# A four-layer vision network on one core: set-up spread out, statistics taken early, norms in steps, and both Toeplitz operands copied in pieces of eight channels

## The chip, the cores and the metric

The kernel runs on one core of one Trainium2 chip. The metric is the device time in microseconds (us) of that core for the whole program. A core has a matrix engine (PE, with its weight loads PEld), a vector engine (DVE), a scalar engine (ACT), a general engine (POOL) and a queue engine that only issues transfers (SP). The profile covers one execution of the same program.

## What is computed

The input is eight images of 56 x 56 positions and 192 channels, all in float32. Four layers follow one another, each of the form `x = x + layer(group_norm(x))`, where the group norm has 32 groups of six channels per image.

```python
# layer 0: gated Toeplitz mixing, 576 inner channels
p, q, v = silu(x @ p_w.T + p_b), silu(x @ q_w.T + q_b), silu(x @ v_w.T + v_b)
a1, a2 = rpe_mlp1(lag) * decay, rpe_mlp2(lag) * decay      # one value per lag and channel
o1 = toeplitz(q * v along w, a1);  o2 = toeplitz(q * v along h, a2)
layer0 = (p * (o1 + o2)) @ o_w.T + o_b
# layer 1: layer norm, then shifted 7 x 7 window attention, 6 heads, bias table and mask
# layer 2: x @ W_in, depthwise 3 x 3, four exponential scans, layer norm, @ W_out
# layer 3: depthwise 7 x 7, layer norm, @ w0, gelu, @ w1, times a small scale
```

A Toeplitz mix of one channel is a 56 x 56 matrix, whose entry depends only on the lag w - w', times a 56 x 56 image of q*v. So layer 0 is 576 pairs of small products per image, one for each direction.

## The kernel before

An image sits in SBUF as 128 partitions: two halves of 28 rows, 64 partitions each, with three chunks of 64 channels in the free dimension (`[128, 3, 1568]`). The program is a row of stages, each over all eight images, and what passes from stage to stage goes through DRAM.

**q and v** (`layer0_qv`, L318 on). For each of 14 slots of an image: matmuls with `w_qv` (L331), bias on DVE (L337), Silu on ACT (L338), product on DVE (L339), and six stores of q*v into two DRAM tables `left` and `right` in runs of 64 channels, or 256 bytes (L342, L347). Group norm of the next image is `layer0_in` (L309): DVE statistics (L149), two small matmuls over the groups (L164), a square root on ACT, and the scaling `xn` (L315). Set-up happens before and between the slots: `toeplitz_rows` (L209) computes the lag coefficients, and each of its 18 blocks reads them back as a sliding window (`hk`, L262, runs of 56 values), reverses them on DVE (`tzt`, L265) and stores them as 64 Toeplitz rows in `left` or `right` (L266). `build_bias_mask` (L271) gathers the bias table with 42 tiny transfers (L280) ahead of the first slot and writes eight mask blocks. The framework that builds the program settles the order of instructions on each engine itself. The trace shows it: the text spreads the 18 blocks over six images, yet the 18 `tzt` copies lie between 77 and 421 us, and only at 422 us is the norm of the fourth image made.

**Mixing** (`layer0_mix`, L442). A block is 64 channels of one image; per image there are nine. Its left and right operands (`lt`, `rt`, 1.79 MB each, L363) stack the Toeplitz rows and the q*v rows so that one product over 128 partitions yields o1 + o2 of one channel. A row holds position and channel, `w * 64 + d`, so the 56 values of one channel lie 64 values (256 bytes) apart. `layer0_operands` (L353) copies the left operand on POOL into `lc`, where a channel is contiguous, in halves of 32 channels (L368); the right operand is read where it lies:

```python
rc = raw[1].rearrange("p (w u d) -> p u d w", u=nu, d=64 // nu)[:, :, nh * q:nh * q + nh]
nc.tensor.matmul(op[64*u:64*u + W, i, :], lc[:, nh*u + d0 + i], rc[:, u, d0 + i], start=True, stop=True)
```

`layer0_products` (L375) does eight products (x `nu`, the number of output halves used together: 2 in eight blocks of an image, 1 in the ninth), and copies them out of PSUM, in turn on DVE (L396) and ACT (L394). After each eight, `between` lets the gate of the pass before go on (`layer0_gate`, L399): p-projection `pj` (L409), Silu (L414), transposes `ot` (L420), gate product (L423), output projection `y` (L430), and the addition into x (L436, L438).

**Layer 1.** `layer1_load` (L547) brings an image in, shifted, in 18 transfers of short runs. `layer1_norm` (L552) is a generator whose first step takes the group statistics of the image; its further steps run between scores and mixing of the image before, by `plan`. `layer1_scores` and `layer1_mix` follow for four groups of windows; the last addition is L717.

**Layer 2.** `layer2_in` (L720): load, statistics (L149, 420 columns at a time), `xn` (L735), 90 matmuls with `w_in` (L747), bias on DVE (L755), one store. `layer2_mix` does the convolution and scans (L791, L806, L807, L815). The output stage takes layer-norm statistics (`ln_pieces`, L187), scales (L862, L864), transposes (L868), projects (`layer2_out`, L883, L888), and after each quarter gives `layer3_in` (L891) a step: statistics of the finished image, norm (`zp`, L900), transposes (L920) and copies (L912, L914).

**Layer 3.** `convolve` (L936) is the 7 x 7 convolution (L956). `layer3_out` (L972) for one image: load `yl`, bias on POOL (L979), 28 layer-norm statistics on DVE (L187), square root on ACT (L202), scaling (L993), transposes (L1000), copy on ACT (L1011), then four rounds of `ph` (L1019), Gelu on ACT (L1023), `po` (L1028), scale on ACT (L1033) and addition (L1035).

Of the kernel before, what the change touches and what calls it, by code (L numbers as in the profile page):

```python
# [76 lines left out]
def kernel(ctx: ExitStack, tc: tile.TileContext, a: dict, out: bass.AP):  # L77
# [43 lines left out]

    left, right = (dram.tile([(nimg * W + 64) * NSUB, QR], F32, name=n) for n in ("left", "right"))
# [15 lines left out]
    def gn_stats_halves(x, pool, psum, sc, sh, ptag="qv"):  # L138

        gn_finish(gn_pieces(x, pool), x.shape[2], pool, psum, sc, sh, ptag)  # L140

    def gn_pieces(x, pool):
        n = x.shape[2]
        nt = -(-n // 512)
        st = pool.tile([128, 3, nt, 6], F32, name="gh_st")
        mv = pool.tile([128, 3, 2], F32, name="gh_mv")
        for j in range(3):
            for t in range(nt):
                nc.vector.bn_stats(st[:, j, t, :], x[:, j, bass.ts(t, n // nt)])  # L149
            nc.vector.bn_aggr(mv[:, j, :], st[:, j].rearrange("p t s -> p (t s)"))  # L150
        return mv

    def gn_finish(mv, n, pool, psum, sc, sh, ptag):
        def over_groups(v, name):
            if ptag == "mm":
                ps = psum.tile([128, 512], F32, name=name, tag="mm", bufs=3)[:, 0:3]
            elif ptag == "gn":
                ps = psum.tile([128, 3], F32, name=name, tag="gn", bufs=1)
            else:
                ps = psum.tile([128, 2, 512], F32, name=name, tag=ptag)[:, 0, 0:3]  # L160
            for j in range(3):
                ks = [k for k in range(3) if abs(j - k) < 2]
                for k in ks:
                    nc.tensor.matmul(ps[:, j:j + 1], gmath[:, k, j, :], v[:, k:k + 1], start=(k == ks[0]), stop=(k == ks[-1]))  # L164
            return ps


        mean = pool.tile([128, 3], F32, name="gh_mean")
        nc.vector.tensor_scalar(mean, over_groups(mv[:, :, 0], "gh_m"), n / NH, None, ALU.mult)
        d = pool.tile([128, 3], F32, name="gh_d")  # L170
        nc.vector.tensor_tensor(d, mv[:, :, 0], mean, ALU.subtract)
        nc.vector.tensor_tensor(d, d, d, ALU.mult)
        nc.vector.tensor_tensor(d, d, mv[:, :, 1], ALU.add)
        if n == NH:
            nc.scalar.activation(sc, over_groups(d, "gh_v"), AF.Sqrt, bias=eps5)
        else:

            z = pool.tile([128, 3], F32, name="gh_z")
            nc.vector.scalar_tensor_tensor(z, mean, 1.0 - n / NH, mean, ALU.mult, ALU.mult)
            nc.vector.scalar_tensor_tensor(z, over_groups(d, "gh_v"), n / NH, z, ALU.mult, ALU.add)  # L180
            nc.scalar.activation(sc, z, AF.Sqrt, bias=eps5)
# [1105 lines left out]
```

## Time and profile before

The time is 6748.18 us, the median of three (6744.67 to 6751.29); the profiled execution spans 6762.3 us. The stages, cut at their first and last matmuls in the trace, and the busy times of the windows that cover them:

| stage | from, to (us) | PE busy | what the windows show |
|---|---|---|---|
| set-up | 0 to 47 | | x arrives at 18, first q/v matmul at 46.7 |
| q and v | 47 to 935 | 765 of 888 us | transfers busy 0.82 to 0.98 of the time |
| mixing | 964 to 2324 | 399 to 400 of every 400 us | PE clock 1.00, POOL 129 to 151 of 400 us |
| layer 1 | 2324 to 3824 | 82 to 85% after the start | PE clock 0.83 to 0.88 |
| layer 2 in | 3824 to 4245 | 83% after the start | DVE 70% |
| layer 2 mix | 4245 to 4885 | nearly 100% | DVE 88% |
| layer 2 out, layer 3 in | 4885 to 5440 | 79 to 86% | DVE 80 to 85% in the first two of its three windows |
| convolution | 5460 to 5765 | | |
| layer 3 out | 5765 to 6762 | 107 of each 120 us in the middle | |

In the page, `busy` counts an engine's own instructions; a busy PE may still be slow per instruction. The forty digits of part 2 show in tenths how busy an engine was in each slice of 169 us. A `<-` names what ended a wait. In matmul rows of the trace a float32 product appears as two records, a transpose as one.

### The profile page before, as it was taken

The page shows a single profiled execution, that of the slowest core. Times are in us where ns is not written, and L with a number is a line of the kernel's source. Part 1 is how long each engine was busy: PE and PEld are TensorE (multiplying, and loading weights), DVE is VectorE, ACT ScalarE, POOL GpSimd, SP SyncE. Part 2 cuts the span into 40 slices and gives each one's busy share as a digit, 9 for nine tenths or more (in the row PEclk, how much of TensorE's full clock was granted, in tenths as well). Part 3 has the DMA queues.
Part 4 walks back from the last instruction along what each step waited for, and adds up shares of the span by engine and source line. Part 5 has one row for each costly group of instructions (what it writes and reads, how often), then busy time and mean ns, then how long its engine had stood idle before and what let it go on. Part 6 is the DMA issues. An engine that isn't in the chain of part 4 may idle for free. (4 is left out here: it accounts for less than half of the span.)

```text
span 6762.3 us, 126227 instructions
## 1 busy us (share of the span) xinstructions
PE 5845.8 (86%) x55962; PEld 3906.1 (58%) x55962; DVE 3297.8 (49%) x4694; ACT 1999.7 (30%) x2784; POOL 1301.5 (19%) x692
## 2 busy tenths in 40 slices
PE   6689989999999778888888588899868889698999
PEld 5567767777777544545454345577534479344444
DVE  6677753333333344444444276688788711532231
ACT  1234431111111133333333100355445410233333
POOL 4210023333333111122121100333301100101000
PEclk8889999999999888888888788999988889799999
DMA  8998895556655434444443554666666588221121
GB/s 193 209 194 176 164 278 206 225 225 225 225 226 224 104 55 59 52 57 53 48 57 44 71 159 164 211 227 233 192 176 191 157 306 318 96 82 51 53 67 26
DMA packets 1041747, 1027.69 MB, mean 152 GB/s; under 512 B 831196, under 2 KB 963716, under 8 KB 1014192
## 3 DMA queue, kind: packets, MB, share of 16 engines
q1 hardware_dynamic: 1028064, 954.30, 50.6%
q0 software_dynamic: 11408, 62.32, 3.7%
q8 instruction: 439, 7.19, 0.4%
q10 hardware_dynamic: 1728, 2.99, 0.1%
q14 instruction: 108, 0.88, 0.0%
HBM read 674.35 MB, written 345.07 MB: 151 GB/s over the span
## 5 line engine op out<-in xcount | busy, mean ns | idle before, releaser
L331 PE MATMUL qv<-w_qv_sb,xn 64*112 64x288 f32 x5376 | 736.1, 428 | 101.4 <-DVE act L337 101.1
L331 PEld LDWEIGHTS qv<-w_qv_sb,xn 64*112 64x112 f32 x5376 | 573.9, 185 | 260.9 <-DVE act L337 127.5
L368 POOL COPY lc<-lt 128x1792 f32<-128x1792 f32 x144 | 473.1, 3289 | 840.0 <-PE op L387 736.8
L387 PE MATMUL op<-rt,lc 128*56 128x56 f32 x9216 | 561.6, 275 | 3.1 <-DMA rt<-right 2.9
L387 PEld LDWEIGHTS op<-rt,lc 128*56 128x56 f32 x9216 | 507.8, 145 | 75.1 <-issue 58.7
L1028 PE MATMUL po<-hid,w_sb 128*64 128x392 f32 x2304 | 400.7, 506 | 69.0 <-ACT hid L1023 69.0
L338 ACT ACTIVATE act<-act 112x576 f32<-112x576 f32 x448 | 301.1, 683 | 507.3 <-DVE act L337 506.7
L1019 PE MATMUL ph<-y,w_sb 64*128 64x392 f32 x2304 | 421.9, 499 | 8.0 <-ACT hid L1023 8.0
L409 PE MATMUL pj<-xn,w_p_sb 64*128 64x392 f32 (+1 forms) x1920 | 370.5, 507 | 25.9 <-DVE xn L451 21.4
L1035 DVE TENSOR_TENSOR x<-x,z 128x392 f32<-128x392 f32 x96 | 54.5, 567 | 654.2 <-ACT z L1033 654.2
L430 PE MATMUL y<-pp,w_o_sb 128*64 128x392 f32 (+1 forms) x1920 | 353.3, 499 | 1.6 <-DVE pp L423 1.2
L423 DVE TENSOR_TENSOR pp<-pp,ot 128x784 f32<-128x784 f32 (+1 forms) x160 | 155.0, 969 | 403.4 <-ACT pp L414 396.3
L1028 PEld LDWEIGHTS po<-hid,w_sb 128*64 128x64 f32 x2304 | 165.6, 140 | 300.3 <-issue 224.6
L791 PE MATMUL cv<-zc,wt 128*128 128x224 f32 x1536 | 312.2, 355 | 28.6 <-DMA zc<-pd 28.6
L337 DVE TENSOR_TENSOR act<-qv,b_qv 112x576 f32<-112x576 f32 x448 | 317.3, 750 | 36.3 <-PE qv L331 36.3
L1019 PEld LDWEIGHTS ph<-y,w_sb 64*128 64x128 f32 x2304 | 232.4, 189 | 172.8 <-issue 25.8
L791 PEld LDWEIGHTS cv<-zc,wt 128*128 128x128 f32 x1536 | 289.9, 189 | 71.7 <-issue 55.9
L660 POOL TENSOR_TENSOR e<-e,mx 128x1176 f32<-128x1176 f32 x64 | 139.9, 2185 | 966.3 <-DVE mx L659 857.5
L610 PE MATMUL qk_ps<-xr,wg 64*96 64x392 f32 x1536 | 309.9, 512 | 14.1 <-ACT qk L616 10.8
L956 PE MATMUL cps<-zc,wt 128*128 128x224 f32 x1536 | 299.0, 355 | 23.4 <-DMA zc<-zd 22.6
L414 ACT ACTIVATE pp<-pj,vecs_sb 128x784 f32<-128x784 f32 (+1 forms) x160 | 146.3, 915 | 568.6 <-PE pj L409 566.5
L747 PE MATMUL pin<-w_in_sb,xn 64*128 64x384 f32 x1392 | 259.6, 521 | 56.9 <-POOL xn L738 36.8
(205 smaller groups left out, 9355.5 us busy)
## 6 DMA issues: line engine op xcount, KB each, us to landing
lt<-left SPq DMA_DIRECT2D x72, 1792.0 KB
rt<-right SPq DMA_DIRECT2D x72, 1792.0 KB
left<-qv SPq DMA_DIRECT2D x224, 252.0 KB
right<-qv SPq DMA_DIRECT2D x448, 126.0 KB
wt<-in_band_dram SPq DMA_DIRECT2D x24, 2048.0 KB
wt<-in_band_dram SPq DMA_DIRECT2D x12, 4096.0 KB
pd<-pt SPq DMA_DIRECT2D x8, 5568.0 KB
zc<-pd SPq DMA_DIRECT2D x192, 232.0 KB
```

The costliest lines, as they stand in the source:

```text
L331: nc.tensor.matmul(ps[s][:, which, 0:D1 // 2], xn[64 * s:64 * s + 64, j, bass.ts(i, 2 * W)], w_qv[64 * s:64 * s + 64, j, which, ns], start ...
L337: nc.vector.tensor_tensor(act, ps[s][:, :, 0:D1 // 2], b_qv[:, :, ns], ALU.add)
L338: nc.scalar.activation(act, act, AF.Silu)
L368: nc.gpsimd.tensor_copy(lc.rearrange("p (u d) w -> p u d w", u=nu), raw[0].rearrange("p (w u d) -> p u d w", u=nu, d=64 // nu)[:, :, nh * ...
L387: nc.tensor.matmul(op[64 * u:64 * u + W, i, :], lc[:, nh * u + d0 + i], rc[:, u, d0 + i], start=True, stop=True)
L409: nc.tensor.matmul(ps[0:M, s, 0:TT], w_p[64 * s:64 * s + 64, j, d0:d0 + M], xn[64 * s:64 * s + 64, j, ts], start=(j == 0), stop=(j == 2),)
L430: nc.tensor.matmul(y[64 * s:64 * s + 64], w_o[0:M, c, 64 * j:64 * j + 64], pp[0:M, s], start=(c == gated[0][0]), stop=(c == gated[-1][0]),)
L610: nc.tensor.matmul(ps[s], wg[64 * s:64 * s + 64, j, c0:c0 + HC], xw[64 * s:64 * s + 64, j, gs], start=(j == 0), stop=(j == 2),)
L791: nc.tensor.matmul(dst, wt[:, c4 + i, 128 * q:128 * q + 128], zc[:, :, c4 + i, q:q + NPAIR], start=(q == 0), stop=(q == 1),)
L956: nc.tensor.matmul(dst.rearrange("p (b n) -> p b n", n=NPAIR), wt[:, c4 + i, q * OP:(q + 1) * OP], zc[:, :, c4 + i, q:q + NPAIR], start=(q ...
L1019: nc.tensor.matmul(ps[:, s, 0:TT], w0[64 * s:64 * s + 64, j, m * 128:(m + 1) * 128], y[64 * s:64 * s + 64, j, ts], start=(j == 0), stop=(j ...
L1028: nc.tensor.matmul(ps[64 * s:64 * s + 64], w1[:, m, 64 * j:64 * j + 64], hid[:, m, s], start=(m == 0), stop=(m == 5),)
```

## The change

The change has four parts.

1. **Set-up spread.** The lag coefficients are computed by a generator, two steps a slot, in image 0. They are transposed on PE and stored in DRAM with the lag as the slow dimension and 64 channels contiguous, so that a Toeplitz row is one contiguous run of 56 x 64 values. The `hk`/`tzt` blocks are gone: 112 transfers from DRAM to DRAM (nine runs of 14,336 bytes each) make the rows and 16 make the zero rows, all issued by ACT, one or two per slot. The bias table's 42 transfers move to slot 10 of image 0 and the eight mask blocks to later slots.
2. **Statistics early.** The group statistics of layer 1 are taken by `gn_piece` in layer 0's last gate, those of layer 2 after each of layer 1's four `layer1_mix` calls; the group averages of seven images come in one call, the eighth's in another. `layer1_norm` and `layer2_in` then only read scale and shift. Layer 1's first two images are loaded before the last gate of layer 0, and the raw operand buffers stand on the other side of SBUF so that they are there before the q/v stage ends.
3. **Norms in steps.** `layer3_in` is cut into more steps, given after each projection chunk of `layer2_out`; the layer-norm pieces are spread likewise. `layer3_out` is split: `layer3_norm` of the next image is a generator, given a step after every second Gelu of the current image, and its variance (DVE) and its square root (ACT) are separate steps. Loads run an image further ahead.
4. **Both operands copied.** The right operand is copied as well, now in pieces of eight channels (x `nu`), in turn on DVE and ACT (`rc`, three buffers); the left operand stays on POOL, in the same pieces (`lc`, two buffers).

The core of the diff:

```diff
-            hk = pool.tile([W, 64, W], F32, name="hk")
-            nc.gpsimd.dma_start(hk, bass.AP(src.tensor, src.offset, [[1, W], [112, 64], [1, W]]))
-            nc.vector.tensor_copy(_reversed(tz[0:W].rearrange("p w d -> p d w")), hk)
-            nc.gpsimd.dma_start((left, right)[i][toep_row(s):toep_row(s) + 64], tz.rearrange("p w d -> p (w d)"))
+        def row(i, w0):
+            nc.scalar.dma_start(
+                parts[i][w0], coef[i][:, 55 - w0:111 - w0].rearrange("s l d -> s (l d)")
+            )
+        def zeros(i, k):
+            nc.scalar.dma_start(parts[i][k], none.partition_broadcast(NSUB))
...
-        nc.gpsimd.tensor_copy(
-            lc.rearrange("p (u d) w -> p u d w", u=nu),
-            raw[0].rearrange("p (w u d) -> p u d w", u=nu, d=64 // nu)[:, :, nh * q:nh * q + nh],
-        )
-        rc = raw[1].rearrange("p (w u d) -> p u d w", u=nu, d=64 // nu)[:, :, nh * q:nh * q + nh]
+    def layer0_operand(copy, raw, name, bufs, d0, nu, pool):
+        c = pool.tile([128, 2, 8, W], F32, name=name, bufs=bufs)
+        copy(c[:, 0:nu], raw.rearrange("p (w u d) -> p u d w", u=nu, d=64 // nu)[:, :, d0:d0 + 8])
+        return c
...
+                for at in range(0, 64 // nu * len(subs), 8):
+                    right_operand()
+                    layer0_products(ops[n % 2], nu, lcs[n], rcs[n])
+                    left_operand()
+                    part = 64 * (nu - 1) + W
+                    copies[n % 2](o[0:part, :, at:at + 8], ops[n % 2][0:part].rearrange("p d h -> p h d"))
+                    n += 1
+                    between()
...
+            if g == len(PASSES) - 1:
+                gn_piece(st, x, t)
+        loaded()
...
-        gn_stats_halves(x.rearrange("p j h w -> p j (h w)"), pool, psum, sc, sh, "mm")
-        yield
+        sc, sh = scsh1[:, b, 0], scsh1[:, b, 1]
...
-        gn_stats_halves(x.rearrange("p j h w -> p j (h w)"), pool, psum, sc, sh, "pin")
+        sc, sh = scsh2[:, b, 0], scsh2[:, b, 1]
...
+        for n in range(0, NPAIR, 4):
+            yield
+            ln_pieces(st, yl, range(n, n + 4))
+        rows = ln_var(st, OP, C, pool)
+        yield
+        rs, mr = ln_rows(*rows, OP, eps6, pool)
         for i0 in range(0, PH, 4):
+            yield
...
                 nc.scalar.activation(hid[:, m], ps[:, :, 0:TT], AF.Gelu, bias=vec("b0", m))
+                if m % 2:
+                    between()
```

## The prediction

> **What bounds the kernel now.** I read the page's slices first, then windows stage by stage, because each stage has its own limit.
>
> ```profile
> PE   6689989999999778888888588899868889698999
> PEclk8889999999999888888888788999988889799999
> DMA  8998895556655434444443554666666588221121
> ```
>
> PE is above 80% nearly everywhere, so what counts is where PE waits and how fast its instructions are. The windows (an image of q/v with Toeplitz blocks, one without, mixing, layer 2 in, layer 3 out) show the stages:
>
> ```profile
> core 0: us, PE busy (x) PEld busy (x) DVE busy (x) ACT busy (x) POOL busy (x), PEclk, DMA share, GB/s
> 111.00:272.00 161.00, 109.16 (x688) 87.47 (x686) 101.82 (x158) 40.46 (x59) 45.37 (x26) 0.84 0.97 202
> 422.00:521.00 99.00, 92.77 (x704) 69.34 (x702) 74.42 (x137) 40.47 (x59) 0.75 (x2) 0.93 0.90 192
> 1000.00:1400.00 400.00, 398.57 (x4556) 293.63 (x4558) 131.07 (x185) 67.05 (x93) 143.18 (x44) 1.00 0.61 235
> 3895.00:4050.00 155.00, 128.07 (x702) 78.10 (x704) 110.22 (x143) 0.89 (x3) 7.60 (x18) 0.86 0.57 173
> 5944.00:6064.00 120.00, 107.14 (x617) 53.84 (x615) 34.98 (x76) 40.23 (x51) 10.35 (x4) 0.94 0.19 64
> ```
>
> An image of q/v lasts 161 us with transfers busy at 0.97, 99 us without blocks. Mixing is PE alone. In the other two PE has gaps; the list of waits on PE names them:
>
> ```profile
> PE gh_m L164 <- DVE gh_mv L150: 113.4, 7, 57.0
> PE qv L331 <- DVE act L337: 101.1, 27, 17.3
> PE po L1028 <- ACT hid L1023: 69.0, 6, 11.9
> PE gh_v L164 <- DVE gh_d L173: 68.6, 23, 7.7
> ```
>
> Two are group-norm chains. The third is a queue effect, in the timeline of layer 3 out:
>
> ```profile
> 5977.78 0.32 ACT L202 ACTIVATE ln_rs<-ln_var,eps 128x28 f32<-128x28 f32 x1 [13.64 <-DVE ln_var L200]
> ...
> 5980.38 0.92 PE L1028 MATMUL po<-hid,w_sb 128*64 128x392 f32 x2 [11.76 <-ACT hid L1023]
> ```
>
> The square root for the next image stands in ACT's queue ahead of a Gelu and waits 13.6 us for its variance; PE waits 11.8 us behind it.
>
> For mixing I looked at the products (PE's timeline, with two outputs in turn, then with one):
>
> ```profile
> 1472.05 3.34 PE L387 MATMUL op<-rt,lc 128*56 128x56 f32 x64
> 1475.32 0.88 PE L430 MATMUL y<-pp,w_o_sb 64*64 64x392 f32 x4
> ...
> 1611.32 1.72 PE L387 MATMUL op<-rt,lc 128*56 128x56 f32 x16
> 1612.96 1.26 PE L409 MATMUL pj<-xn,w_p_sb 64*128 64x392 f32 x6
> ```
>
> From start to next start: 3.27/64 = 51 ns a record in pairs, 1.64/16 = 102 ns alone. The convolution L956 has 256 records in 49.5 us, 193 ns for 224 columns that lie in runs, 0.86 ns a column; at that rate 56 columns take 48 ns. Alone they take twice that, and only the right operand is read at a stride.
>
> **What the Trainium skill says.** "Advanced Engine Details and Errata", section Memory Cachelines: SBUF lines are 16 bytes and a read that meets a new line each time is penalized. The trace agrees: 102 against 48 ns at a 256-byte step. "TensorE: Matmul & The Clock Gate", section LDWEIGHTS: a weight load takes its columns / 1.2 ns, 107 ns for 128; the 14 `gh_m` records of 128 columns and one moving column took 1.72 us, 123 ns each, which fits. By it 56 columns take 47 ns, a possible floor (estimate). "SBUF — State Buffer", section on the two sides: POOL and a DVE copy in its fast mode lock each other out for a whole instruction. The trace fits: L315 takes 1.09 us alone, and one group of three 5.96 us. "DMA: Bandwidth & Descriptors", section on why a DMA increments by 16: the number of engines is the largest divisor up to 16 of the slowest dimension. A row transfer has nine; no transfer before shows it.
>
> **The change, part by part.**
>
> *Set-up and q/v (0 to 935).* The coefficient chain and bias table leave the path to the first matmul: `xn` ends at 35.8, the first matmul is at 46.7. The blocks' sliding reads (18 x 784 KB in 224-byte runs) and `tzt` (18 x 3.23 = 58 us of DVE) go. Images without blocks took 99, 96, 96 and 88 us, and the last 23 slots 134.4, which is 82 per 14. Added are 128 transfers of 126 KB each, issued by ACT. An ACT issue took about 0.45 us at the start and 0.9 for `coef`: 58 to 115 us on ACT, which is busy 320 of 888; Silu waits behind it, DVE's product behind Silu. As transfer time: 16.5 MB on nine of 16 engines; the loads `lt` and `rt` ran at up to 384 GB/s on 16 (window 935 to 1000), so 24 GB/s an engine gives 76 us over the stage, 10 an image, on engines that are 0.83 to 0.9 busy already. I take 98 an image: 36 + 7 x 98 + 82 = 804, rounded to 810: **-125** (-145 if the transfers hide, -20 if they don't). The mask blocks are only moved; they hide in DVE's 25% slack. Operands loaded early shorten the 29 us to the first product: **-10**.
>
> *Products.* With both operands contiguous, one record alone should take max(48, weights 47) plus the transposes' 10 ns of overhead, 57. In pairs PE ran two column groups at once (51 = 102/2); the bounds are 28 (half of 57) and 49 (weight loads in a row). The nearest row, `v_ps` with 64-column weights in four quadrants, has 94 records in 2.30 us, 24 ns, which a strict row of loads within a row group (53/2 = 27) would not allow. I take 35. Pairs: 8192 records x 16 = -132. Alone: 1024 x 45 = -46. The copies: 320 pieces, 896 values in pairs. POOL's 3289 ns for 1792 gives 1.65 each, 256 x 1.65 + 64 x 0.9 = 480 us as before. On DVE 0.9 ns a value (`tzt`) to 2.0 (`zt`, 1084 for 512): 0.8 to 1.8 us; ACT likewise (`zt` 1090). 160 pieces each add 130 to 290 us to DVE's 452 and to ACT's 233: both below the new stage of 1200. But `lc` has two buffers: piece n+2 can be copied only after products n; and DVE copies queue ahead of the gate's L423, behind which `y` on PE waits, with shorter products to cover it. 160 gate chunks x 0.25 us = +40. Net **-138**.
>
> *Statistics early.* Layer 1's start (2324 to 2418): x arrives at 2359, stats and chain end at 2373; both now lie under the last gate: **-48**. In its body 28 matmuls an image go (3.4 us of PE, and some 1.6 of waits), seven times: **-35**; DVE trades one set of 12 statistics for another. Layer 2 in: an image takes 43.9 us ((4243+3-3895)/8), PE's matmuls 174 x 0.161 = 28, DVE's additions 15 x 1.53 = 23 plus 3.3 for `xn`. Without 12 x 0.575 of statistics and the chain (PE idle or on `gh` from 3931 to 3942) PE bounds it at 30: **-105**, and the first chain **-12**; its load still waits for the 18 stores (SP issues for 40 us).
>
> *Steps.* Layer 2 out: about 66 us an image, DVE 53, PE 52. ACT waited 13.4 us for `gh_v` in one image, PE 6.7 for `gh_d`. Nothing is removed; I take 60: **-50** (0 to -75). Layer 3 out: the last image, whose norm was made before, takes 105. Five images fall from 120 to 104.5 and the first from 138: **-110**. DVE (35 us an image) and ACT (40) have room.
>
> Sum: -125 -10 -138 -48 -35 -105 -12 -50 -110 = -633; 6748 - 633 = **6115**.
>
> **Rivals.** *Weight loads bound the products*: pairs stay at 49, saving 17 + 46 - 40 = 23 instead of 138: 6230. For it, the 123 ns of `gh_m`; against it, `v_ps`. *Transfers still bound q/v*: nine engines get all rows, or ACT's queue holds up Silu: -20 instead of -125, 6220. For it, 0.90 without blocks. *Everything overlaps*: pairs at 28 with no give-back (-230 instead of -138), q/v -145, layer 2 out -75, and some 15 more from the rest: 5960. *Slower*: the buffers make mixing a series. A group of 1.1 us of products, then a left copy that waits for a DVE copy (1.65 + 1.85), then its gate (104 us an image / 40 = 2.6) is 7.2 us x 320 = 2300 instead of 1358: +942 against -495 of the rest: 7195. For it, the shared port and two buffers; against it, POOL is busy only 36% and a gate step lies between most groups.
>
> **The numbers.** The forecast 0.45, weight loads 0.18, transfers 0.12, everything 0.18, slower 0.07. The range runs from the best case to the weight-load case plus 80 for the open sizes of the steps: 5960 to 6310. Faster 0.92, same 0.01, slower 0.07.
>
> **What would show it.** The first L331 near 36; q/v images near 98 with transfers near 0.9; L387 at 35 ns a record in pairs and 57 alone, with PE still at 0.95 or more in mixing; no `gh` rows in layer 1's and layer 2's images; L747 every 30 us; no ACT wait for `ln_var` and 104 us an image at the end. It would be wrong if PE waits for `rc` or `lc`, if pairs stay near 50, or if ACT's queue stands in its own transfers.

## The result and the profile after

The changed kernel takes 6349.33 us (median of 6344.86 to 6358.06), the kernel before 6749.74 beside it: a ratio of 0.9408, 95% interval 0.9392 to 0.9425. That is 400 us less, where the prediction had 633 and ended its range at 6310. The direction held and the size did not. Cut at the same first and last matmuls as before, the profiled spans (6762.3 and 6349.2) divide like this:

| term of the prediction | before (us) | after (us) | forecast | measured |
|---|---|---|---|---|
| set-up and q/v, 0 to the last `qv` | 935.2 | 867.3 | -125 | **-68** |
| last `qv` to the first product | 29.3 | 7.7 | -10 | -22 |
| mixing, first to last product | 1331.6 | 1194.4 | -138 | -137 |
| layer 1 start, last product to first `qk` | 121.5 | 100.2 | -48 | **-21** |
| layer 1, first `qk` to last `pr` | 1405.9 | 1387.6 | -35 | -18 |
| last `pr` to the first `pin` | 71.3 | 56.1 | -12 | -15 |
| layer 2 in, first to last `pin` | 348.2 | 242.8 | -105 | -105 |
| layer 2 out, first to last `po` | 475.5 | 475.8 | -50 | **0** |
| layer 3 out, first `ph` to last `po` | 948.5 | 923.9 | -110 | **-25** |

Part 2 of the page of the changed kernel, the span in 40 slices (of 159 us now):

```profile
PE   6799989999999688888888598999588798789999
PEclk8899999999999888888888799999798799899999
DMA  6799886666665613444433675666667488121211
```

The windows answer to those shown of before: an image of q/v in which mask blocks are made, one late in the stage, mixing, layer 2 in, layer 3 out. The columns are the window, its length, the busy time of the five engine rows, the PE clock, the transfers' busy share and GB/s.

```profile
core 0: us, PE busy (x) PEld busy (x) DVE busy (x) ACT busy (x) POOL busy (x), PEclk, DMA share, GB/s
228.00:325.00 97.00, 71.30 (x439) 59.16 (x441) 56.37 (x131) 24.43 (x37) 17.02 (x29) 0.81 0.69 168
616.00:713.00 97.00, 95.58 (x762) 71.42 (x760) 73.85 (x132) 43.83 (x65) 0.00 (x0) 0.96 0.93 207
1300.00:1700.00 400.00, 379.53 (x5190) 249.76 (x5188) 244.81 (x312) 166.92 (x163) 201.80 (x110) 0.98 0.71 267
3613.00:3768.00 155.00, 154.67 (x912) 109.47 (x913) 129.85 (x95) 0.00 (x0) 13.19 (x31) 0.98 0.88 264
5770.00:5885.00 115.00, 107.89 (x620) 53.78 (x619) 35.18 (x77) 40.01 (x51) 10.71 (x4) 0.96 0.20 67
```

Late in q/v PE is full with the transfers at 0.93, and layer 2 in is bound by PE, as forecast. Three rows are not as forecast. In the first, PE is idle for a quarter of the time and DVE, ACT and transfers are all less busy than in the second: something makes them wait for one another. In mixing PE is no longer full (0.95), and its clock is 0.98. In layer 3 out PE has 107.9 of 115 us.

The list of waits on PE puts names to the idle time (total, times, longest):

```profile
PE ph L1087 <- ACT hid L1091: 49.1, 6, 10.0
PE qv L366 <- DVE act L372: 47.6, 19, 5.5
PE po L926 <- DVE x2o L931: 46.1, 8, 9.8
```

The second was 101.1 before. Waits for `hid` were 69.0 before, at `po`, and should have gone; in the prediction's words "no ACT wait for `ln_var`". The third was 17.6: it has grown. Each is read in a timeline below.

The products, from PE's timeline, first with one output, then with two in turn:

```profile
1310.64 0.99 PE L412 MATMUL op<-rc,lc 128*56 128x56 f32 x16
1311.56 2.25 PE L424 MATMUL pj<-xn,w_p_sb 64*128 64x392 f32 x12
...
1336.74 1.86 PE L412 MATMUL op<-rc,lc 128*56 128x56 f32 x64
1338.53 1.53 PE L445 MATMUL y<-pp,w_o_sb 64*64 64x392 f32 x8
```

From start to next start: 0.92/16 = 57.5 ns alone (102 before) and 1.79/64 = 28 ns in pairs (51 before). At these rates the products gained 8192 x 23 + 1024 x 45 = 234 us, and mixing, 137 us shorter, gave 97 back. Counting each matmul record up to the start of the next one shows where: the products took 314 us of PE where they took 532 (16 less than the 234, since not every group runs at the full rate), the two projections of the gate 664 where they took 647, the small matmuls of layer 1's statistics, which now lie here, 5, and PE's idle time grew from 7.5 to 66 us. So 59 of the 97 are idle time of PE.

### The profile page after: what moved, and what is told of

It reads as the page before. It is cut to its first block, busy times and chain, and to the rows that moved or that the text cites. A ratio compares the mean times of both kernels' runs of the same rounds, so it can differ in the third digit from the quotient of the medians.

```text
span 6349.2 us, 126376 instructions
## 1 busy us (share of the span) xinstructions
PE 5569.1 (88%) x55636; PEld 3587.9 (57%) x55636; DVE 3439.3 (54%) x4752; ACT 2239.7 (35%) x2922; POOL 1302.1 (21%) x813
## 5 line engine op out<-in xcount | busy, mean ns | idle before, releaser
L366 PE MATMUL qv<-w_qv_sb,xn 64*112 64x288 f32 x5376 | 722.2, 425 | 50.9 <-DVE act L372 47.6
L404 POOL COPY lc<-lt 128x896 f32<-128x896 f32 (+1 forms) x320 | 573.0, 1808 | 616.7 <-PE op L412 598.7
L366 PEld LDWEIGHTS qv<-w_qv_sb,xn 64*112 64x112 f32 x5376 | 535.5, 184 | 232.8 <-DVE act L372 64.7
L1087 PE MATMUL ph<-y,w_sb 64*128 64x392 f32 x2304 | 429.9, 511 | 49.1 <-ACT hid L1091 49.1
L1098 PE MATMUL po<-hid,w_sb 128*64 128x392 f32 x2304 | 395.1, 496 | 10.8 <-ACT hid L1091 10.8
L412 PEld LDWEIGHTS op<-rc,lc 128*56 128x56 f32 x9216 | 308.4, 136 | 127.6 <-issue 65.7
L412 PE MATMUL op<-rc,lc 128*56 128x56 f32 x9216 | 339.7, 222 | 46.0 <-POOL lc L404 24.2
L404 ACT COPY rc<-rt 128x896 f32<-128x896 f32 (+1 forms) x160 | 256.9, 1606 | 230.7 <-PE op L412 216.0
L1009 PEld LDWEIGHTS cps<-zc,wt 128*128 128x128 f32 x1536 | 290.0, 189 | 32.5 <-issue 24.9
L847 POOL TENSOR_TENSOR rows<-rows,loc 128x896 f32<-128x896 f32 x96 | 228.1, 2377 | 390.2 <-ACT rows L843 262.8
```

The lines of the kernel that those rows point to most:

```text
L366: nc.tensor.matmul(ps[s][:, which, 0:D1 // 2], xn[64 * s:64 * s + 64, j, bass.ts(i, 2 * W)], w_qv[64 * s:64 * s + 64, j, which, ns], start ...
L404: copy(c[:, 0:nu], raw.rearrange("p (w u d) -> p u d w", u=nu, d=64 // nu)[:, :, d0:d0 + 8])
L412: nc.tensor.matmul(op[64 * u:64 * u + W, i, :], lc[:, u, i], rc[:, u, i], start=True, stop=True)
L1009: nc.tensor.matmul(dst.rearrange("p (b n) -> p b n", n=NPAIR), wt[:, c4 + i, q * OP:(q + 1) * OP], zc[:, :, c4 + i, q:q + NPAIR], start=(q ...
L1087: nc.tensor.matmul(ps[:, s, 0:TT], w0[64 * s:64 * s + 64, j, m * 128:(m + 1) * 128], y[64 * s:64 * s + 64, j, ts], start=(j == 0), stop=(j ...
L1098: nc.tensor.matmul(ps[64 * s:64 * s + 64], w1[:, m, 64 * j:64 * j + 64], hid[:, m, s], start=(m == 0), stop=(m == 5),)
```

## Experiments

Ratios are to the kernel before on the same chip; the changed kernel has 0.9408. Stage times are from each kernel's own trace, and they are what the verdicts rest on, since layer 1, which none of the edits is meant to shorten past its start, took from 1370 to 1404 us in these profiles at a granted clock of 0.85 to 0.87.

**Layer 3 out: the place of the square root.** In the changed kernel's timeline, in order of time over three engines:

```profile
5561.34 5.92 DVE L189 BATCH_NORM_STATS2 ln_st<-yl 128x6 f32<-128x192 f32 x14
...
5572.33 0.32 ACT L209 ACTIVATE ln_rs<-ln_var,eps 128x28 f32<-128x28 f32 x1 [7.11 <-DVE ln_var L203]
...
5574.38 1.72 ACT L1091 ACTIVATE hid<-ph,vecs_sb 128x784 f32<-128x784 f32 x2
5575.35 9.85 PE L1087 MATMUL ph<-y,w_sb 64*128 64x392 f32 x48 [7.70 <-ACT hid L1091]
```

The text gives each norm a step after every second Gelu, with the root in the third of four rounds of an image. The trace has all 28 statistics nearly in one go and the root in the first round, ahead of the Gelus: the framework that builds the program had moved them up. The root waits 7.1 us for the variance, the Gelus stand behind it, PE waits 7.7. (In ACT's timeline a table load of 1.28 us precedes the root and another the Gelu after it, the second inside PE's wait.) The edit only fixes the root's place; `pin` is true for layer 3's norm alone:

```diff
-        nc.scalar.activation(rs, var, AF.Sqrt, bias=eps[0:P])
+        root = nc.scalar.activation(rs, var, AF.Sqrt, bias=eps[0:P])
+        if pin:
+            tc.keep_in_program_order(root)
```

> The changed kernel with one edit: the square root of layer 3's next norm (ln_rows in layer3_norm) is kept on ACT behind the instruction that the text puts ahead of it, so it can't be moved up. Theory A (the framework moves the root up to the first Gelus of an image, where it waits 6.5 to 8.0 us for the variance and PE waits 7.7 us behind it, then runs 48 matmuls in 9.85 us where 8.1 is usual): the 7.7 and the 1.8 us go in each of the six images that have a root, so an image takes 104 to 106 us where it takes 115, layer 3 out shrinks from 924 to about 865, and the time falls from 6349 to about 6292. Theory B (the root is late because the load and POOL's additions are late; its place in the queue is not the cause): the wait stays or moves with it, an image stays at 112 to 115 us, 6335 to 6350.

Measured: 6252.36 us, ratio 0.9275 (0.9258 to 0.9291). The stage went from 923.9 to 846.8 us, an image takes 105 us, and PE's wait for `hid` is 0.5 us in all. A window of that kernel:

```profile
5545.00:5650.00 105.00, 105.00 (x620) 52.80 (x618) 35.38 (x76) 40.12 (x51) 10.71 (x4) 1.00 0.23 73
```

Same work, but PE busy throughout and the clock at 1.00 where it was 0.96. Theory A holds, and it won 77 us where I had allowed 57. The 60 us of waits for `hid` (49.1 at `ph`, 10.8 at `po`) are gone; the other 17 fit the slower matmuls after a wait, 48 in 9.85 us above where a round of the new kernel takes 72 in 12.12. The granted clock of the changed kernel shows it: in the wait, in the 4.7 us behind it, and after that (the last column but two).

```profile
5570.00:5575.00 5.00, 0.00 (x0) 0.00 (x0) 4.93 (x16) 2.65 (x4) 0.00 (x0) 0.69 0.18 39
5575.30:5580.00 4.70, 4.65 (x18) 2.63 (x20) 2.15 (x6) 1.48 (x2) 0.00 (x0) 0.63 0.68 183
5580.00:5585.20 5.20, 5.20 (x34) 2.74 (x32) 0.00 (x0) 2.06 (x3) 0.00 (x0) 1.00 0.86 362
```

Eighteen records are in the second window and 34 in the third. The table loads are all still there, seven before roots and eight before Gelus in this stage of either kernel; in their new place PE does not wait for them.

**q/v: mask blocks in DVE's queue.** The text gives each image one mask block or two. In the trace all eight lie between 232 and 301 us, and the additions stand in DVE's queue waiting for their loads, with the bias additions behind them:

```profile
270.99 1.73 DVE L326 TENSOR_TENSOR bmt<-mk,bt 128x196 f32<-128x196 f32 x6 [6.54 <-DMA mk<-in_mask_dram]
...
273.00 0.75 DVE L372 TENSOR_TENSOR act<-qv,b_qv 112x576 f32<-112x576 f32 x1
...
273.81 5.67 PE L366 MATMUL qv<-w_qv_sb,xn 64*112 64x288 f32 x24 [4.62 <-DVE act L372]
```

Seven such waits add up to 35.1 us on DVE. Cut from every 672nd `qv` matmul to the next, the eight images of the changed kernel, numbered 0 to 7, take 137, 141, 97, 100, 98, 90, 89 and 82 us (the expectations below have them about a microsecond shorter). The edit moves the additions to the engine that issues the loads:

```diff
-                nc.vector.tensor_tensor(
+                nc.gpsimd.tensor_tensor(
                     bm[:, h % 3, :, h // 3, :], mk, bt[:, h:h + 1, :].to_broadcast([128, 4, WN]), ALU.add
```

> The changed kernel with one edit: the 48 additions of bias and mask (bmt) run on POOL, not on DVE. Theory A (DVE's queue stands in seven additions that wait 35.1 us for mask loads, and PE waits 27.7 us behind the bias additions queued after them): those waits go, the second image of q/v takes 97 to 105 us where it takes 139, and the time falls by 30 to 42, to 6307 to 6320. Theory B (PE in this stretch is held by the transfers or by ACT, or POOL's additions hold DVE up in their turn): the second image stays at 130 or more, 6340 to 6355.

Measured: 6317.07 us, ratio 0.9371 (0.9356 to 0.9387). Image 1 takes 100 us instead of 141 and image 2 108 instead of 97; PE's waits behind the bias additions fell from 47.6 to 26.9 us, and the last `qv` comes at 835.0 instead of 867.3. Theory A, 32 us.

**q/v: the coefficient chain in image 0.**

```diff
+        for _ in coefs:
+            pass
...
-                for i in range(PH):
-                    between[i].insert(0, lambda: [next(coefs, None) for _ in range(2)])
```

> The changed kernel with the lag coefficients made in one go ahead of image 0, not in two steps a slot. Theory A (the chain between the slots is what makes image 0 take 136 us where 97 are usual: PE waits 12.9 us for cps, 6.2 for qv, and runs at a clock of 0.70 to 0.85 until 146): the first matmul moves back to about 47, image 0 takes 95 to 105, q/v ends 15 to 28 us earlier, 6321 to 6334. Theory B (image 0 is slow for other reasons: the first loads, the next image's statistics on DVE, the tiny bias transfers): image 0 stays above 125 and the 12 us at the start come on top: 6355 to 6365.

Measured: 6343.65 us, ratio 0.9412 (0.9393 to 0.9431): no change. The first matmul moved from 34.2 to 46.3, image 0 fell from 137 to 113, and images 1 to 4 took the other 12 us back (100 and 105 for images 2 and 3): the last `qv` came at 867.0. Neither theory held as it was put: the chain between the slots does cost image 0 some 24 us, but moving it ahead of the images won nothing. With the four edits that won (below) it was tried again:

> The four edits of the last kernel, and the lag coefficients made in one go ahead of image 0. Alone that edit took 24 us from image 0, put 12 at the start, and images 2 and 3 took 9 more between them, so that q/v ended where it had. Theory A (with the mask additions off DVE the later images keep their length: 12 us are won): ratio 0.918 to 0.920 to the kernel before, where the four edits have 0.921. Theory B (rows that start earlier lengthen the later images whatever DVE does): within 0.0015 of 0.921, or above.

Measured: ratio 0.9218 (0.92 to 0.9236), theory B. Image 0 is 23 us shorter and starts 12 later, and images 2 to 4 take 113, 106 and 102 us where they took 108, 100 and 97. The number of rows is not why: the two kernels issue 9, 24, 24, 24, 24, 7 and 10, 23, 25, 24, 24, 6 row transfers in images 0 to 5. In images 2 to 4 PE's waits behind the bias additions grew from 22.0 to 35.1 us and Silu's waits for stores of q*v to land from 13.8 to 30.5; why stays open.

**q/v: what a row transfer costs.** Two runs were meant to price it.

```diff
-            nc.scalar.dma_start(
-                parts[i][w0], coef[i][:, 55 - w0:111 - w0].rearrange("s l d -> s (l d)")
-            )
+            for _ in range(2):
+                nc.scalar.dma_start(
+                    parts[i][w0], coef[i][:, 55 - w0:111 - w0].rearrange("s l d -> s (l d)")
+                )
```

> The changed kernel with each of the 112 Toeplitz-row transfers made twice, to the same place. In the changed kernel images of q/v with rows take 96 to 99 us, those without 89. Theory A (the transfers cost PE about 7 us an image, through the queues that the stores of q*v share, or through ACT, which issues each in 0.69 us): another 5 to 8 us an image over the first five or six, q/v longer by 25 to 45, 6375 to 6395. Theory B (the rows hide; images 2 to 4 are longer for the norms and the loads): q/v within 8 us, 6345 to 6357.

Measured: 6423.85 us, ratio 0.9531 (0.9514 to 0.9547), q/v 79 us longer. It doesn't price the row: a second transfer to the same place waits for the first to land, ACT stood in 22 such waits for 138 us, up to 9.8 in one, with Silu behind it, and the transfers' busy share fell (0.91 to 0.83 after image 1). Neither theory was tested. The second run changed the issuing engine:

```diff
-            nc.scalar.dma_start(
+            nc.gpsimd.dma_start(
                 parts[i][w0], coef[i][:, 55 - w0:111 - w0].rearrange("s l d -> s (l d)")
```

> The changed kernel with one edit: the 112 Toeplitz-row transfers are issued by POOL, not by ACT. Doubling them cost 79 us of q/v, 0.71 us a transfer, which is an ACT issue's 0.69, while the transfers' busy share fell. Theory A (their price is ACT's issue time, behind which Silu, DVE's product and PE stand): images 3 to 6 of q/v fall from 96 to 99 towards 89 us, q/v shrinks by 25 to 50, 6300 to 6325. Theory B (the price is the traffic itself, whoever issues it): q/v stays within 10 us, 6340 to 6355. Theory C (POOL's issues and its hold on the path that it shares with DVE cost more than ACT's): q/v grows, above 6360.

Measured: 6346.72 us, ratio 0.9366 (0.935 to 0.9383). q/v is 20 us shorter, but not for the reason of theory A: images 2 to 5 take 98, 107, 94 and 92, 391 us together where they had 384, and image 0 takes 147. What fell is image 1, 141 to 104: the mask blocks, whose loads POOL issues among its rows, now lie between 234 and 550 us, and DVE's waits for their loads fell from 35.1 to 3.1 us. That is a second sign for the mask reading. Taking ACT's 0.69 us an issue away won nothing in images 2 to 5. What a row transfer costs stays open: neither run priced it.

**Layer 1 start: a store behind early loads.** SP's and ACT's timeline of the changed kernel:

```profile
2058.78 53.81 SPq L593 DMA_DIRECT2D x<-x  x36
2112.69 1.24 SPq L476 DMA_DIRECT2D x<-x  x2
...
2126.21 5.83 ACT L614 ACTIVATE xr<-x,scsh 128x392 f32<-128x392 f32 x9 [33.01 <-DMA x<-x]
```

The early loads of two images take SP 54 us to issue, and the store of layer 0's last image (L476), ready at 2097, stands behind them. The first `xr` and a memset of `e` on POOL (at 2126.22, after 24.77 us) start together, which points to that store landing: `e` needs no load, and layer 1's buffers take the space of mixing's.

```diff
-            x.extend(layer1_load(b, xpool) for b in range(min(2, nimg)))
+            x.append(layer1_load(0, xpool))
...
         layer0_mix(pool, blocks, psum, ops, w_p, w_o, loaded)
+        x.extend(layer1_load(b, x[0]) for b in range(1, min(2, nimg)))
```

> The changed kernel with one edit: only layer 1's first image is loaded ahead of layer 0's last gate; the second is loaded after the last store of layer 0. Theory A (layer 1's first norm waits until 2126 because its buffer takes the place of layer 0's last image, whose store stands on SP behind 36 early loads: the addition ends at 2098 and the store is issued at 2113): the store goes out near 2099, the first xr starts at 2108 to 2114, and layer 1 starts 12 to 18 us earlier: 6331 to 6338. Theory B (the first norm waits for its own load): xr starts at 2120 or later and the time stays within 5 us of 6349.

Measured: 6315.01 us, ratio 0.9367 (0.9352 to 0.9382). The store is issued at 2096, the first `xr` starts at 2110.5, and layer 1 starts 87.8 us after the last product instead of 100.2: theory A. (Another 14 us of the difference in time lie in layer 1, at a clock of 0.87 where it had 0.85.)

**Layer 2 out: who sets the pace.** The wait that took the place of the old one, on DVE and then PE:

```profile
4748.47 13.12 DVE L189 BATCH_NORM_STATS2 ln_st<-ml 112x6 f32<-112x384 f32 x17
4761.52 0.66 DVE L931 SCALAR_TENSOR_TENSOR x2o<-po,vecs_sb,x2o 128x448 f32<-128x448 f32 x1
...
4762.23 4.52 PE L926 MATMUL po<-y,w_out_sb 128*64 128x448 f32 x12 [5.62 <-DVE x2o L931]
```

The text gives three or four statistics after each projection chunk; the queue has 17 in a row, ahead of the addition that frees PE's buffer. The edit keeps each in its place, for this stage:

```diff
-            nc.vector.bn_stats(st[:, n], yl[:, :, n])
+            piece = nc.vector.bn_stats(st[:, n], yl[:, :, n])
+            if pin:
+                tc.keep_in_program_order(piece)
```

> The changed kernel with one edit: the layer-norm statistics of layer 2's output stage (ln_pieces in between) are kept on DVE behind the instruction that the text puts ahead of them, so three or four follow each projection chunk and no run of 17 can form. Theory A (the run of 13 us stands ahead of the addition that frees PE's buffer; PE waits 46.1 us for it, and this has taken the place of the 35.0 us for gh_v): these waits fall below 15 us, the stage from the first to the last po shrinks from 476 to 435 to 450, 6310 to 6325. Theory B (DVE, 0.77 busy with some 53 us an image, or the chain of norm, transposes and copies sets the pace, and the waits only change their name): 465 to 480 for the stage, 6338 to 6352.

Measured: 6328.05 us, ratio 0.9395 (0.9375 to 0.9414). PE's wait for `x2o` fell from 46.1 to 20.7 us, but that for `zt` grew from 5.0 to 15.8, and the stage shrank by 11 us, to 464.8: at the edge of theory B's range. Whether the pace is DVE's work was then asked by taking the statistics away:

```diff
-                if b + 1 < nimg and i < 8:
+                if b + 1 < nimg and i == 0:
+                    nc.vector.tensor_copy(ml[b + 1][1], ml[0][1])
+                if b + 1 < nimg and i < 0:
                     ln_pieces(ml[b + 1][1], ml[b + 1][0], range(NPAIR * i // 8, NPAIR * (i + 1) // 8))
```

> The changed kernel with layer 2's layer-norm statistics left out for images 1 to 7, image 0's being copied for them (the output is not the reference's): 196 statistics of 0.78 us, 153 us of DVE's 383 in the stage. Theory A (DVE's work sets the pace of layer 2 out): the stage, 476 us from the first to the last po, falls by 60 to 130. Theory B (the chain from scaling over transposes, ACT's copies and projection sets it, and the statistics only fill gaps): it falls by less than 30.

Measured: the stage falls from 475.8 to 403.6, ratio 0.9273 (0.9246 to 0.93). With 153 us of work less on DVE, 72 us are won, and PE is busy for 387 of 404 us: theory A. Putting DVE's work in finer steps won 11.

**Mixing: where the 97 us went.** First the right copies were left out altogether, and the product reads `raw` at a step again:

```diff
-    rcs.append(layer0_operand(copies[i % 2], blocks[i][1], "rc", 3, d0, nu, pool))
+    rcs.append(
+        blocks[i][1].rearrange("p (w u d) -> p u d w", u=nu, d=64 // nu)[:, :, d0:d0 + 8]
+    )
```

> The changed kernel with the right operand's copies left out: the products read it in place at a step of 64 values, as in the kernel before; the left operand still comes in pieces of eight channels. Theory A (the copies shorten a product from 51 to 28 ns in pairs and from 102 to 57.5 alone, worth 8192 x 23 + 1024 x 45 = 234 us, and the copies give some 97 back in waits of PE and a lower clock): products return to 51 and 102 ns, the waits vanish, mixing goes from 1194 back to 1320 to 1340 and the time to 6475 to 6495. Theory B (the give-back comes from the small pieces of the left operand and not from the right copies): the waits for lc stay and mixing goes past 1370, the time past 6520. Theory C (the products were not held by the step of the right operand): mixing stays below 1250, the time below 6410.

Measured: 6498.68 us, ratio 0.9639 (0.9619 to 0.966); products at 51 to 52 ns in pairs and 103 alone, PE 0.998 busy at clock 1.00 in the middle of the stage, mixing 1358.5. Theory A in kind, though mixing is 27 us longer than in the kernel before. The products are not why (533 us of PE where they took 532): 9 us are idle time of PE, 12 the first projection of the gate and 5 the matmuls of layer 1's statistics. Why that projection took longer I don't know. Then two tries to end PE's waits by moving the copies. The first puts all right copies on ACT; the second gives the left copies the third buffer (and makes them ahead of the products, the right ones after).

```diff
-    rcs.append(layer0_operand(copies[i % 2], blocks[i][1], "rc", 3, d0, nu, pool))
+    rcs.append(layer0_operand(nc.scalar.copy, blocks[i][1], "rc", 3, d0, nu, pool))
```

> The changed kernel with all 320 right-operand copies on ACT, none on DVE. Theory A (DVE and POOL hold each other up: POOL's left copy takes 2008 ns, where half of the copy before took 1645; the gate and the copies queue on DVE): POOL's copies fall to 1650 to 1800 ns, PE's waits for lc and x fall from 41 to under 20 us, mixing shrinks by 15 to 35, 6314 to 6334. Theory B (ACT, 0.40 busy, now gets 226 us more at 1765 ns a piece, and the Silu of the gate waits behind the copies): PE waits for pp instead, mixing grows by 20 or more, above 6370.

```diff
-    layer0_operand(copies[i % 2], blocks[i][1], "rc", 3, d0, nu, pool)
+    layer0_operand(copies[i % 2], blocks[i][1], "rc", 2, *todo[i][2:], pool)
...
-    layer0_operand(nc.gpsimd.tensor_copy, blocks[i][0], "lc", 2, *todo[i][2:], pool)
+    layer0_operand(nc.gpsimd.tensor_copy, blocks[i][0], "lc", 3, d0, nu, pool)
...
-                    right_operand()
+                    left_operand()
                     layer0_products(ops[n % 2], nu, lcs[n], rcs[n])
-                    left_operand()
+                    right_operand()
```

> The changed kernel with the third buffer moved from the right operand's copies to the left's: lc has three, rc two, and the left copy of two pieces ahead stands before the products, the right one after them. Theory A (PE's 24.2 us behind POOL's lc, in 36 waits, come of lc's two buffers: a left copy of 1.7 to 2.0 us can start only when the products two pieces back are done): the lc wait falls below 8 us, the rc wait grows by less than that, mixing 8 to 20 us shorter, 6329 to 6341. Theory B (the copies' own times set it, and two buffers on the right cost what three on the left save): PE's waits for the two together stay at 35 to 60 us, mixing within 8 us or longer.

Measured: mixing 1195.0 and 1207.2 (ratios 0.9431, 0.9414 to 0.9449, and 0.9406, 0.9387 to 0.9424). PE's waits changed their names, and their sum did not fall: with `rc_act` 24.7 us for `lc`, 18.4 for `rc` from ACT, 13.8 for `pp`; with `lc3_rc2` none for `lc`, but 46.6 for `x` and 16.5 for `rc`. No theory held whole. With `lc3_rc2` the wait for `lc` went as in A, without the gain; with `rc_act` POOL's large copies fell from 2011 to 1792 ns as in A, the wait for `pp` came as in B, and mixing stayed. Then each side was cut to one copy a block:

```diff
-    rcs.append(layer0_operand(copies[i % 2], blocks[i][1], "rc", 3, d0, nu, pool))
+    rcs.append(
+        rcs[-1] if d0 else layer0_operand(copies[i % 2], blocks[i][1], "rc", 3, d0, nu, pool)
+    )
```

> The changed kernel with most right-operand copies left out: a block's first piece is used for all its products, so DVE and ACT make 72 copies where they made 320, with the products at the same rate (the output is not the reference's). Theory A (the right copies in DVE's and ACT's queues, some 226 us each, hold back gate and left copies): mixing falls from 1194 by 55 to 100, to 1095 to 1140. Theory B (POOL's left copies set the waits): mixing stays at 1170 to 1200, PE waits for lc.

```diff
-    lcs.append(layer0_operand(nc.gpsimd.tensor_copy, blocks[i][0], "lc", 2, *todo[i][2:], pool))
+    lcs.append(
+        lcs[-1] if todo[i][2]
+        else layer0_operand(nc.gpsimd.tensor_copy, blocks[i][0], "lc", 2, *todo[i][2:], pool)
+    )
```

> The changed kernel with most left-operand copies left out: a block's first piece is used for all its products, so POOL makes 72 copies where it made 320 (the output is not the reference's). Theory A (the right copies on DVE and ACT cost the time): the 24 us for lc go, others come for them, mixing 1170 to 1195. Theory B (POOL's copies, and what they take from DVE by the shared path, cost it): mixing falls by 55 to 100, to 1095 to 1140, and DVE's right copies fall below 1534 ns.

Measured: mixing 1164.7 without most right copies (-30) and 1139.4 without most left ones (-55); ratios 0.9348 (0.9296 to 0.94) and 0.9304 (0.9277 to 0.9332). The first lies between its theories, the second is its theory B: both sides cost, POOL's more, and its 55 us include PE's 24 of waits for `lc`. The groups of costliest instructions show the rest. DVE's right copies in the changed kernel (count, then busy time and mean ns):

```profile
L404 DVE COPY rc<-rt 128x896 f32<-128x896 f32 (+1 forms) x159 | 225.4, 1424 | 27.3 <-DMA rt<-right 18.1 <-PE op L412 9.2
```

and with POOL's copies nearly gone:

```profile
L404 DVE COPY rc<-rt 128x896 f32<-128x896 f32 (+1 forms) x158 | 169.9, 1079 | 41.3 <-DMA rt<-right 23.8 <-PE op L412 10.9 <-PE pj L424 6.3
```

On average the same copy takes three quarters of the time when POOL rests. The timeline of the changed kernel shows why:

```profile
1333.19 4.16 POOL L404 COPY lc<-lt 128x896 f32<-128x896 f32 x2 [0.58 <-PE op L412]
1333.57 2.16 DVE L404 COPY rc<-rt 128x896 f32<-128x896 f32 x1
...
1337.88 0.94 DVE L404 COPY rc<-rt 128x896 f32<-128x896 f32 x1
1337.92 4.21 POOL L404 COPY lc<-lt 128x896 f32<-128x896 f32 x2 [0.57 <-PE op L412]
```

Whichever starts second stands until the first is done. Of DVE's 127 large copies (896 values), the 16 that meet no POOL instruction take 0.91 to 0.96 us. Of the 71 that start inside a left copy, 65 end 0.78 to 0.87 us after it, however long it still had to run, and DVE's longest takes 2.92. The other way round, 65 of the 66 large left copies that start inside a large right copy end 1.6 us after it, where a left copy that meets no DVE instruction takes 1.73. ACT's right copies take 1.76 us in both kernels. So the left copies went to ACT and all right ones to DVE:

```diff
-    layer0_operand(copies[i % 2], blocks[i][1], "rc", 3, d0, nu, pool)
+    layer0_operand(nc.vector.tensor_copy, blocks[i][1], "rc", 3, d0, nu, pool)
...
-    layer0_operand(nc.gpsimd.tensor_copy, blocks[i][0], "lc", 2, *todo[i][2:], pool)
+    layer0_operand(nc.scalar.copy, blocks[i][0], "lc", 2, *todo[i][2:], pool)
```

> The changed kernel with the left operand's 320 copies on ACT and the right operand's 320 on DVE, none on POOL. Theory A (POOL at work holds DVE up; without it a right copy takes 1079 ns): DVE is busy some 120 us longer, ACT some 250, both below 0.75 of mixing, and mixing falls by 20 to 50, to 1145 to 1175, ratio 0.933 to 0.938. Theory B (the number of copies in two queues that also carry the gate is what counts): PE waits for pp and for lc behind ACT's Silu, mixing 1190 or longer, ratio 0.940 or above.

Measured: 6335.26 us, ratio 0.9358 (0.934 to 0.9376); a right copy takes 870 ns on average, 320 of them 275.5 us, mixing 1180.5. The ratio is in theory A's range; the gain of 14 us in mixing is less than A had, and mixing lay between 1187 and 1207 us in the profiles that copied all operands otherwise.

**Together.** The four edits `l3_pin`, `masks_pool`, `l1_one` and `l2o_pin`, and then these with `lc_act`:

> The changed kernel with four edits together: the root of layer 3's norm kept in its place on ACT, the bias and mask additions on POOL, only one image of layer 1 loaded early, and layer 2's statistics kept in their places on DVE. Theory A (the four lie in separate stages and add up: layer 3 out 77, q/v 32, layer 1's start 12, layer 2 out 11): 6349 - 132 = 6217, a ratio of 0.917 to 0.925 to the kernel before. Theory B (one takes back what another gives, by the clock or by a reordered queue): above 6260.

> The four edits of the combination (layer 3's root, masks on POOL, one early load, layer 2's statistics in place) and the left copies on ACT, the right ones on DVE. Theory A: what the last kernel wins in mixing adds to the four edits, ratio 0.921 less 0.003 to 0.007, 0.914 to 0.918. Theory B: 0.920 or above.

Measured: ratios 0.9209 (0.9193 to 0.9225) and 0.9167 (0.9152 to 0.9182). Theory A for both: the four edits add up (0.9408 - 0.9209 is 134 us of 6750), and `lc_act` adds its 14 us of mixing (1200.5 to 1186.3). The last kernel beats both others: 6209.21 us beside 6771.63, about 2.6% below the changed kernel (0.9167/0.9408).

## Why the prediction was wrong

- **Layer 3 out**, forecast -110, measured -25: the largest miss. The failed step is "its variance and square root are separate steps", taken to mean that ACT no longer waits for the variance. The size was right: with the root kept in its place an image takes 105 us (forecast 104.5) and the stage is 102 us shorter than before. I had written myself, of the 18 `tzt` copies, that the framework settles the order on each engine, and did not apply it to the new steps.
- **Set-up and q/v**, -125 against -68. Two steps failed: "the mask blocks are only moved; they hide in DVE's 25% slack" (their wait for loads, not their work, stood in the queue: 32 us by `masks_pool`) and 98 us for image 0 as for the others (137; the coefficient chain is 24 of it). For images 2 to 6 98 was a fair figure: 97 to 100, then 90. The rival "transfers still bound q/v" (-20) is not what happened, but how much the row transfers cost stays open.
- **Layer 2 out**, -50 against 0. The failed step is "I take 60" an image. PE's wait at `gh_v` went from 35.0 us to 6.5, as meant, but DVE had 53 us of work in a 66 us image and nothing was removed; the wait came back as `x2o`. The stage got 72 us shorter when DVE's statistics went and 11 when they were only put in order, so DVE, busy for 378 of 476 us, was the bound already, though PE was busier (397).
- **Layer 1 start**, -48 against -21: "both now lie under the last gate" left out the queue. The early loads also stand ahead of a store whose buffer the first norm needs. One image's loads less won 12 us; the other 15 stay open.
- **Mixing**, -138 against -137, is a hit by luck, of two errors that cancel. Pairs went to 28 ns, the lower bound, not 35 (-188, not -132), and the give-back was 97, not 40. I had priced it as 160 gate chunks x 0.25; the trace has 59 us more idle time of PE, 17 in the gate's projections, 16 in products below the full rate and 5 in statistics. Of the waits that the price names, the one for `lc` came to 24 us and that of `y` behind the gate product (`pp`, L423 before) to 1.2; the waits for `rc` (17.5) and for the additions into x (17.3) it put at nothing, and it has no term for POOL's and DVE's copies holding each other up. Its own sign of being wrong, PE waiting for `rc` or `lc`, came true. The rival of weight loads (49 ns in pairs) is out with 28 ns. By the figure that the prediction took from "TensorE: Matmul & The Clock Gate", section LDWEIGHTS, 47 ns for 56 columns (an estimate), two loads in a row would take 94 ns, and two products went through in 56; so the loads for the two halves overlap, if the estimate holds.
- **Layer 2 in** was right to the us (30.4 us an image, PE 154.67 of 155), as were its start and the gap before mixing or better. **Layer 1's body**, -35 against -18, can't be judged: 1370 to 1404 us in the profiles covers both.

Of the 222 us missed (633 less the 411 that the stages add up to), 85 are layer 3 out, 57 q/v, 50 layer 2 out, 27 layer 1's start and 17 its body, less 14 for the gap and the small terms. An edit shows the cause of the first and the third, of 32 us in q/v and of 12 in layer 1's start. Of image 0's excess over 98, 24 us are put down to the coefficient chain, but no kernel won them; the rest of layer 1's start and its body stay open.

## What to carry to other kernels

When a change spreads work "in steps", ask not whether the engine has room but what each in-order queue will hold: an instruction moved ahead of its input, here a square root waiting for its variance and additions waiting for their loads, holds up everything behind it. Read the order from the trace, and where the builder may reorder, fix the place of the few instructions that wait. And an engine that is 80% busy with in-order pieces can be the bound of a stage while another is busier by the profile: here DVE, 378 of 476 us against PE's 397.

## What the runs showed of the hardware

- A wait cost PE more than its length. In layer 3 out 60 us of waits for `hid` went and 77 us were won, with the clock of the windows from 0.96 to 1.00. "TensorE: Matmul & The Clock Gate", Part 1, "The HAM clock gate", says that the clock follows how busy PE has lately been; the trace agrees: after a wait of 7.7 us the granted clock was 0.63 for 4.7 us and then 1.00, and 48 matmuls took 9.85 us where 8.1 is usual (12.12 x 48/72).
- POOL's and DVE's copies of SBUF held each other up, each for the whole of the other's instruction: a large right copy took 0.94 us where it met no POOL instruction and up to 2.92 beside one. It is the lock that the prediction took from "SBUF — State Buffer", section on the two sides. With POOL's copies nearly gone the mean of all sizes fell from 1424 to 1079 ns, with none to 870. Its price in the stage was small: `rc_act` and `lc_act`, which each keep the two apart, won nothing and 14 us, since ACT took on the copies.
- Products that alternate between the two output halves went through in 28 ns each, 57.5 for one half alone: twice the rate, weight loads included. With the moving operand read at a step of 256 bytes it was 51 and 102.
